# Scan stage of a four-layer image network: whole decays in PSUM, channel-group order, transposed attention

## The chip, the cores and the metric

The kernel runs on one core of one Trainium2 chip, in one launch. Its metric is the device time of that core in microseconds. Three executions of the kernel before took 13820.34 to 13844.27 us, median 13823.51; one further execution was profiled.

## The reference

64 images of 128 channels x 28 x 28 pixels (784 positions) in fp32 pass through four layers.

- Layer 0: two quantised 3x3 convolutions, each with a batch norm over all 64 images.
- Layer 1: attention inside each image. `scores = q^T k` (16 rows deep, 784 x 784), softmax along each row, values times weights, `gamma * out + x`.
- Layer 2: a Mamba block over the 784 positions of an image, in four reading directions: `h = exp(d*A)*h + d*u*B` for 160 inner channels x 24 states, `y = sum_n C*h`, plus `D*u`, times `silu(z)`, an output product, a mixing product, a residual.
- Layer 3: a small Mamba block over 8 tokens inside every pixel, group norm, silu, residual.

## The kernel before

`conv_block` runs first: batch norm needs all images before layer 1 may begin. `attention_and_mamba` (layers 1 and 2, here called the scan stage) follows, then `token_mamba` (layer 3). The change is in the scan stage alone.

**Units.** One image's scan has 160 x 24 = 3840 rows of 784 positions, 30 tiles of 128 partitions: a unit holds 32 channels (channel group q of NQ = 5) times 4 states (state group g of NG = 6). Units run in the order g outer, q inner (`at(n)`). For each unit:

- `inject` (GpSimd): `h = ur * Br`, the rows of d*u for group q, each on 4 x 32 partitions, times the rows of B for group g. It runs AHEAD = 5 units early; the h tiles number 10.
- `decay` (ScalarE): `a = exp(A * dr)`.
- `scan` (VectorE): one `tensor_tensor_scan` runs the recurrence along 784 positions. For q = 1 and 3 (`whole`) the decay lies in SBUF, up to three units ahead, and one instruction does 784; for q = 0, 2, 4 the decay is made in halves of 392 in PSUM (tile `ah`, 2 buffers) and two scans follow each other in `ah`.
- product with C: GpSimd for q = 1, 3 in g < 5 (10 of 30 units), VectorE for the others, in halves where the scan was.
- `sums` (TensorE): `fold` adds the 4 states of each channel into the PSUM tile `y`, which collects an image's 160 channels (channels 0 to 127 as 128 x 784, the last 32 as quarters over the partitions) over all six g. At the end VectorE multiplies `y` with the gate z in one instruction (`yo`, in `after`), and the output product follows.

**Rows.** `rows_bc` and `rows_d` fetch the rows of B, C, d and d*u from DRAM, spread over partitions in four transfers of 98 KB each, issued by SyncE. The B and C tiles have 2 buffers and are fetched one g ahead, the d and d*u tiles have 5.

**Side work.** While image b is scanned, three generators advance a few steps per unit (`side`): `attention` two to three images ahead, `inputs` (layer norm, input product, causal convolution as shifted products, softplus, silu) of image b+1, and `after` of image b−1. Attention takes 112 rows of scores at a time in a two-bank PSUM tile `wide`: row maximum (VectorE, `nmax`), exp with its row sum (ScalarE, `e`), seven transposes on TensorE copied out by ScalarE (`et`), the product with `vt` in seven pieces of 128 columns, a scaling copy (`avn`), a transpose back and the residual (`x`).

**Order.** Nothing is issued while this code runs. A `Plan` records each instruction with its reads, writes and pool buffers, `cost` gives each a length, and `Plan.order` lists them by a greedy simulation over five in-order queues (TensorE, VectorE, ScalarE, GpSimd, SyncE), for twelve settings of lead and patience, keeping the shortest; the scan chain has a lower rank (`plan.first()`) and so goes first among what is ready. All instructions are issued from one line, L493, so the profile is read by tile names.

**PSUM.** Eight banks: `bank` 2, `wide` 2, `ah` 2, `y` 2.

## Time and profile before

| | |
|---|---|
| median of 3 runs | 13823.51 us |
| profiled execution | 13818.13 us (span 13816.2) |
| granted TensorE clock, mean | 0.845 |
| VectorE busy | 12431.7 us (90%) |
| GpSimd busy | 11433.1 us (83%) |
| ScalarE busy | 10845.5 us (78%) |
| TensorE busy | 10467.5 us (76%) |
| DMA | 1297.64 MB, 94 GB/s |
| first nmax of the scan stage / last yo | about 683 us / 7738.4 us |

Engines are written PE (TensorE), PEld (its weight loads), DVE (VectorE), ACT (ScalarE), POOL (GpSimd) and SP (SyncE). A group's line names engine, operation, output tile `<-` input tiles, shapes and count, then busy time and mean length, then idle time of the engine just before such instructions and what ended it. A product of fp32 data stands as two matmul records. Lengths of neighbouring instructions of one engine overlap a little, since the next begins while the last one drains. Shares over the whole span mix three stages: the stretch from 3000 to 6000 us is the scan stage alone.

### The profile page before, as it was taken

Reading aid. Unit: us, or ns where it says so; the run is one execution under the profiler, and the core shown is the slowest. Engines: PE = TensorE matmul, PEld = TensorE weight load, DVE = VectorE, ACT = ScalarE, POOL = GpSimd, SP = SyncE. Lnnn points to the kernel's source line nnn. Section 1 sums busy time; section 2 is a strip of 40 time slices with the busy share of each in tenths; the row PEclk is TensorE's granted clock in tenths of the full one; section 3 lists DMA queues with packets and bytes.
Section 4 is the critical chain, followed back from the end, with each engine's and each line's share of the span. In section 5 each row is a group of like instructions: output and inputs, shape, how many; then the busy total and the mean of one; then the engine's idle time right before and its main releaser. Section 6 shows DMA issues by size and latency. Waiting matters only on the chain. (4 is left out here: it accounts for less than half of the span.)

```text
span 13816.2 us, 181376 instructions
## 1 busy us (share of the span) xinstructions
PE 10467.5 (76%) x58370; PEld 7153.8 (52%) x58370; DVE 12431.7 (90%) x12740; ACT 10845.5 (78%) x25904; POOL 11433.1 (83%) x5304
## 2 busy tenths in 40 slices
PE   9877777777777777777777577777767677777776
PEld 9644444444444444444443355656556565565564
DVE  3569999999999999999999799999999999999998
ACT  2367777777777777777777688888888888888887
POOL 0058999888988889898889788888888888888887
PEclk9988888888888888888888788888888888888887
DMA  3534444444444444444443211111111111121111
GB/s 129 186 93 128 124 125 125 133 126 126 123 125 130 129 125 122 126 126 132 129 122 120 74 49 54 51 52 60 44 54 49 56 56 46 51 63 46 52 51 46
DMA packets 711515, 1297.64 MB, mean 94 GB/s; under 512 B 206624, under 2 KB 357536, under 8 KB 710560
## 3 DMA queue, kind: packets, MB, share of 16 engines
q1 hardware_dynamic: 710560, 1286.05, 30.5%
q8 instruction: 460, 7.54, 0.2%
q14 instruction: 495, 4.06, 0.1%
HBM read 954.72 MB, written 330.76 MB: 93 GB/s over the span
## 5 line engine op out<-in xcount | busy, mean ns | idle before, releaser
L493 ACT ACTIVATE a<-delta,A 128x98 f32<-128x98 f32 x14336 | 3905.0, 366 | 764.7 <-PE y L493 545.2
L493 POOL TENSOR_TENSOR h<-ur,Br 128x784 f32<-128x784 f32 x1920 | 4196.7, 2211 | 138.9 <-PE y L493 122.0
L493 POOL TENSOR_TENSOR db<-u,BC 128x896 f32<-128x896 f32 x1568 | 3275.8, 2114 | 131.6 <-DVE h L493 125.5
L493 PE MATMUL y<-a,ident 128*128 128x280 f32 x7168 | 2059.4, 452 | 702.3 <-DVE a L493 701.2
L493 DVE TENSOR_TENSOR_SCAN ah<-ah,h 128x392 f32<-128x392 f32 x2304 | 2303.6, 1000 | 60.7 <-ACT ah L493 49.2
L493 PEld LDWEIGHTS y<-a,ident 128*128 128x128 f32 x7168 | 1554.0, 220 | 1223.4 <-issue 406.4
L493 DVE TENSOR_TENSOR_SCAN h<-a,h 128x784 f32<-128x784 f32 x768 | 1917.7, 2502 | 97.3 <-ACT a L493 54.2
L493 ACT ACTIVATE ah<-dr,A 128x392 f32<-128x392 f32 x2304 | 1322.7, 587 | 617.0 <-DVE ah L493 604.3
L493 POOL TENSOR_TENSOR h<-h,Cr 128x784 f32<-128x784 f32 x640 | 1362.0, 2132 | 354.2 <-DVE h L493 342.1
L493 DVE TENSOR_TENSOR h<-h,a 128x896 f32<-128x896 f32 x1344 | 1476.6, 1099 | 43.0
L493 DVE TENSOR_TENSOR h<-ah,Cr 128x392 f32<-128x392 f32 x2304 | 1302.6, 565 | 72.8
L493 PE MATMUL y<-h,fold 128*32 128x98 f32 (+1 forms) x12288 | 1023.3, 420 | 392.5 <-DVE h L493 366.7
L493 DVE TENSOR_TENSOR h<-h,db 128x896 f32<-128x896 f32 x1120 | 1230.3, 1098 | 94.1 <-POOL db L493 11.4
L493 PEld LDWEIGHTS bank<-vt,et 112*112 112x112 f32 x6272 | 892.1, 212 | 235.7 <-ACT et L493 88.7
L493 DVE TENSOR_TENSOR a<-h,BC 128x896 f32<-128x896 f32 x896 | 976.8, 1090 | 28.8
L493 PE MATMUL bank<-vt,et 112*112 112x128 f32 x6272 | 968.3, 317 | 6.6 <-ACT et L493 2.8
L493 POOL TENSOR_TENSOR xn<-s,sq 128x784 f32<-128x784 f32 x64 | 135.8, 2122 | 873.5 <-ACT sq L493 808.3
L493 PEld LDWEIGHTS y<-h,fold 128*32 128x32 f32 x12288 | 383.3, 121 | 910.4 <-DVE h L493 436.8
L493 PEld LDWEIGHTS y<-late,ident 128*128 128x128 f32 x7168 | 832.4, 192 | 23.2 <-issue 6.5
L493 ACT ACTIVATE a<-dr,A 128x784 f32<-128x784 f32 x768 | 716.9, 942 | 154.9 <-DVE h L493 147.9
L493 PE MATMUL y<-late,ident 128*128 128x112 f32 x7168 | 836.5, 274 | 0.0
L493 POOL TENSOR_TENSOR a<-a,db 128x896 f32<-128x896 f32 x224 | 530.0, 2366 | 309.6 <-issue 239.4
(212 smaller groups left out, 20910.5 us busy)
## 6 DMA issues: line engine op xcount, KB each, us to landing
Br<-bcd SPq DMA_DIRECT2D x1536, 98.0 KB, 2.4
Cr<-bcd SPq DMA_DIRECT2D x1536, 98.0 KB, 2.4
dr<-dud SPq DMA_DIRECT2D x1280, 98.0 KB, 2.3
ur<-dud SPq DMA_DIRECT2D x1280, 98.0 KB, 2.3
utd<-tok SPq DMA_DIRECT2D x128, 392.0 KB, 2.8
ztd<-tok SPq DMA_DIRECT2D x128, 392.0 KB, 3.7
rows<-utd SPq DMA_DIRECT2D x192, 256.0 KB, 2.9
xt<-in_x SPq DMA_DIRECT2D x32, 784.0 KB, 4.9
```

Of the source, the lines that this page charges most:

```text
L493: last = getattr(getattr(nc, engine), method)(*args, **kw)
```

## The change

- Units run q outer, g inner. The row tiles follow: all six B and all six C tiles stay for an image (6 buffers each), the d and d*u tiles have 2.
- Every decay is a whole one of 784 in a PSUM tile `a` of two banks, 2 buffers, made one unit ahead; every scan is one instruction. Where VectorE multiplies with C, the state stays in `a`; where GpSimd does, the scan writes `h` in SBUF. GpSimd takes g = 1, 3 and, for q = 1, 3, g = 5: 12 of 30 units. The h tiles number 9.
- `y` is one bank with the 32 channels of one q as four quarters; after the six g of a q, VectorE multiplies it with z (now laid out by q) into its piece of `yo`. The output product takes `yo` in 20 pieces, 64 rows deep, with the packed weight `Wout`.
- Attention: q and k get a 17th row, k's of ones. A first pass of scores gives row maxima in halves (`mx`), whose negatives (`nm`) go through a transpose, ScalarE and DRAM into q's 17th row. A second pass computes the scores transposed, already less the maxima, so that exp (`et`) yields the weights in the layout that the product with `vt` needs: seven products of 392 columns for each half. Row sums come from products with ones (`den`), reciprocals as exp(−ln) (`rq`), spread by products with `first_row` (`rd`). The bias of v is added at the end with the residual (`gbv`).
- PSUM: `bank` 3, `a` 4, `y` 1. The planner's costs for TensorE columns and GpSimd elements go from 0.0023 to 0.0021 us.

The diff, cut to its core; the removed lines of attention and sums are among the functions above.

```diff
         if engine == "tensor":
             if kw.get("is_transpose"):
                 return 0.18, False, 0.25
-            if outs[0].partition_size() == 32 or ins[0].partition_size() == 16:
+            if outs[0].partition_size() == 32:
+                return max(0.1, 0.03 + 0.0005 * n), False, 0.25
+            if ins[0].partition_size() in (16, 17):
                 return 0.03 + 0.0005 * n, False, 0.25
...
-        plan = Plan(tc, 0.0023, 0.0023, True)
+        plan = Plan(tc, 0.0021, 0.0021, True)
...
-        pss = plan.pool(ctx.enter_context(tc.tile_pool(name="pss3", bufs=1, space=PSUM)), 1)
-        psb = plan.pool(ctx.enter_context(tc.tile_pool(name="psb3", bufs=2, space=PSUM)), 2)
-        psh = plan.pool(ctx.enter_context(tc.tile_pool(name="psh3", bufs=1, space=PSUM)), 1)
+        psb = plan.pool(ctx.enter_context(tc.tile_pool(name="psb3", bufs=3, space=PSUM)), 3)
+        psa = plan.pool(ctx.enter_context(tc.tile_pool(name="psa3", bufs=2, space=PSUM)), 2)
         psy = plan.pool(ctx.enter_context(tc.tile_pool(name="psy3", bufs=1, space=PSUM)), 1)
-        def wide_psum():
-            return pss.tile([C, 2, 512], F32, name="wide")
...
+            x0 = p2.tile([C, T], F32, name="x0")
             plan.vector.tensor_scalar(x0, raw, MAGIC, 1.0 / 15.0, ALU.subtract, ALU.mult)
...
+            qt = p1.tile([49, T], F32, name="qt")
+            kt = p1.tile([49, T], F32, name="kt")
+            k0 = VEC_AT["bk"][0]
             for h in range(2):
...
+                acc = bank()[:113, :HT]
+                product(acc, [(w("WqkT"), x0[:, HALF[h]])])
+                act(qt[:, HALF[h]], acc[0:49], AF.Identity, bias=v("bq", p=49))
+                act(kt[:, HALF[h]], acc[64:113], AF.Identity, bias=vec[64:113, k0 : k0 + 1])
+            yield
...
+            rows16 = [slice(32 * h, 32 * h + 16) for h in range(2)]
+            rows17 = [slice(32 * h, 32 * h + 17) for h in range(2)]
+            mx = p1.tile([TP, NT, 2], F32, name="mx")
+            for i in range(NT):
+                sc = [bank()[:TP, :HT] for h in range(2)]
+                for h in range(2):
+                    plan.tensor.matmul(
+                        sc[h], lhsT=qt[rows16[h], i * TP : (i + 1) * TP], rhs=kt[rows16[h], HALF[h]],
+                        start=True, stop=True,
+                    )
+                for h in range(2):
+                    plan.vector.tensor_reduce(mx[:, i, h : h + 1], sc[h], AX.X, ALU.max)
+                yield
+            nm = p1.tile([TP, NT], F32, name="nm")
+            plan.vector.tensor_reduce(nm, mx, AX.X, ALU.max, negate=True)
+            tr = bank()[:NT, :TP]
+            plan.tensor.matmul(tr, lhsT=nm, rhs=ident[:TP, :TP], start=True, stop=True)
+            nmt = p1.tile([NT, TP], F32, name="nmt")
+            act(nmt, tr, AF.Copy)
+            nmd = rows_dram.tile([NT, TP], F32, name="nmd")
+            plan.sync.dma_start(nmd, nmt)
+            for h in range(2):
+                plan.sync.dma_start(qt[32 * h + 16 : 32 * h + 17, :], nmd.rearrange("(o a) c -> o (a c)", o=1))
+            yield
+            x1 = p2.tile([C, T], F32, name="x1")
+            for h in range(2):
+                et = []
+                for j0 in range(0, NT, 2):
+                    js = range(j0, min(j0 + 2, NT))
+                    sc = [bank()[:TP, :HT] for _ in js]
+                    for j in js:
+                        rows = rows17[j % 2]
+                        plan.tensor.matmul(
+                            sc[j - j0], lhsT=kt[rows, j * TP : (j + 1) * TP], rhs=qt[rows, HALF[h]],
+                            start=True, stop=True,
+                        )
+                    for j in js:
+                        e = p1.tile([TP, HT], F32, name="et", bufs=8)
+                        act(e, sc[j - j0], AF.Exp)
+                        et.append(e)
+                    yield
+                den = bank()[:, :ET]
+                for j in range(NT):
                     with plan.together():
...
+                        for k in range(4):
                             plan.tensor.matmul(
...
+                                den[32 * k : 32 * k + 32], lhsT=ones, rhs=et[j][:, k * ET : (k + 1) * ET],
+                                start=(j == 0), stop=(j == NT - 1), skip_group_check=True,
                             )
...
+                rq = p2.tile([C, ET], F32, name="rq")
+                act(rq, den, AF.Ln)
+                act(rq, rq, AF.Exp, scale=-1.0)
                 yield
...
+                acc = bank()[:, :HT]
+                with plan.together():
+                    for k in range(4):
+                        plan.tensor.matmul(
+                            acc[:, k * ET : (k + 1) * ET], lhsT=first_row[:, k : k + 1].broadcast_to([C, C]), rhs=rq,
+                            start=(k == 0), stop=True, skip_group_check=True,
+                        )
+                rd = p2.tile([C, HT], F32, name="rd")
+                act(rd, acc, AF.Copy)
+                av = bank()[:, :HT]
+                for j in range(NT):
+                    plan.tensor.matmul(av, lhsT=vt[:, j, :], rhs=et[j], start=(j == 0), stop=(j == NT - 1))
+                plan.vector.scalar_tensor_tensor(x1[:, HALF[h]], av, v("att_gamma"), rd, ALU.mult, ALU.mult)
                 yield
...
+            plan.vector.scalar_tensor_tensor(x1, x1, gbv, x0, ALU.add, ALU.add)
             plan.sync.dma_start(x1d[b % 4], x1)
...
-            z = p2.tile([C, 2, HW2], F32, name="z", bufs=3)
+            z = p2.tile([C, NQ, QT], F32, name="z", bufs=3)
...
-            for h in range(2):
-                acc = bank()[:, :HT]
-                product(acc, [(winz[:, :C], shifted[3][:, HALF[h]])])
-                act(z[:, h, :HT], acc, AF.Identity, bias=bias[:, 0, 1:2])
+            for q0 in (0, 2):
+                acc = bank()
+                for k in range(2):
+                    q = q0 + k
+                    quarters(
+                        acc[:, k * QT : (k + 1) * QT], [(winz[:, 32 * q : 32 * q + 32], shifted[3])], first=(k == 0)
+                    )
+                    act(z[:, q, :], acc[:, k * QT : (k + 1) * QT], AF.Identity, bias=biasz[:, q : q + 1])
...
-        def rows_bc(b, g):
+        def rows_bc(b, g, k):
             bcd = given[b][2]
-            for k, name in enumerate("BC"):
-                t = p2.tile([C, T], F32, name=f"{name}r", bufs=2)
-                n = 24 * k + 4 * g
-                spread(t, lambda r: bcd[n + r : n + r + 1, :].broadcast_to([32, T]))
-                rows_of[name, b, g] = t
+            name = "BC"[k]
+            t = p2.tile([C, T], F32, name=f"{name}r", bufs=NG)
+            n = 24 * k + 4 * g
+            spread(t, lambda r: bcd[n + r : n + r + 1, :].broadcast_to([32, T]))
+            rows_of[name, b, g] = t
         def rows_d(b, q, k):
             name = ("dr", "ur")[k]
-            t = p2.tile([C, T], F32, name=name, bufs=NQ)
+            t = p2.tile([C, T], F32, name=name, bufs=2)
             spread(t, lambda r: given[b][3][k, 32 * q : 32 * q + 32, :])
             rows_of[name, b, q] = t
-        def after(b, ys):
-            z = given.pop(b)[1]
+        def after(b, yo):
+            given.pop(b)
...
             for h in range(2):
                 acc = bank()[:, :HT]
-                product_q(acc, h, w("WoutA"), lambda j: w("WoutB", j * C, (j + 1) * C), yo)
+                rows = slice(64 * h, 64 * h + 64)
+                for q in range(NQ):
+                    with plan.together():
+                        for k in range(2):
+                            at = (2 * q + k) * C
+                            plan.tensor.matmul(
+                                acc[:, k * QT : (k + 1) * QT], lhsT=w("Wout", at, at + C)[rows], rhs=yo[rows, q, :],
+                                start=(k == 0 and q == 0), stop=(q == NQ - 1), skip_group_check=True,
+                            )
...
-        def whole(g, q):
-            return q in (1, 3)
+            q, g = divmod(n, NG)
+            return b, g, q
         def on_gpsimd(g, q):
-            return q in (1, 3) and g < 5
+            return g in (1, 3) or (g == 5 and q in (1, 3))
         def inject(n):
             b, g, q = at(n)
             if n == 0:
-                rows_bc(0, 0)
-                for i in range(NQ):
+                for i in range(2):
                     for k in range(2):
                         rows_d(0, i, k)
-            h = hs[n] = st.tile([C, T], F32, name="h", bufs=10)
+                for i in range(NG):
+                    for k in range(2):
+                        rows_bc(0, i, k)
+            h = hs[n] = st.tile([C, T], F32, name="h", bufs=9)
             plan.gpsimd.tensor_tensor(h, rows_of["ur", b, q], rows_of["B", b, g], ALU.mult)
-            if q == 0:
-                nxt = (b, g + 1) if g + 1 < NG else (b + 1, 0)
+            if g == NG - 1:
+                nxt = divmod(b * NQ + q + 2, NQ)
                 if nxt[0] < NB:
-                    rows_bc(*nxt)
-            if g == NG - 1 and b + 1 < NB:
-                rows_d(b + 1, q, 1)
-        def decay(n, hf=None):
+                    rows_d(*nxt, 1)
+            if q == NQ - 1 and b + 1 < NB:
+                rows_bc(b + 1, g, 0)
+        def decay(n):
             b, g, q = at(n)
-            k, dr = g * NQ + q, rows_of["dr", b, q]
-            if hf is None:
-                a = st.tile([C, T], F32, name="a", bufs=4)
-            else:
-                a, dr = psh.tile([C, 512], F32, name="ah", bufs=2)[:, :HT], dr[:, HALF[hf]]
-            decays[n, hf] = a
-            act(a, dr, AF.Exp, scale=A[:, k : k + 1])
-            if hf != 0 and g == NG - 1 and b + 1 < NB:
-                rows_d(b + 1, q, 0)
-        def scan(n, hf=None):
+            k = g * NQ + q
+            a = decays[n] = psa.tile([C, 1024], F32, name="a")[:, :T]
+            act(a, rows_of["dr", b, q], AF.Exp, scale=A[:, k : k + 1])
+            if g == NG - 1:
+                nxt = divmod(b * NQ + q + 2, NQ)
+                if nxt[0] < NB:
+                    rows_d(*nxt, 0)
+        def scan(n):
             b, g, q = at(n)
-            a, h, Cr = decays.pop((n, hf)), hs[n], rows_of["C", b, g]
-            since = 0.0
-            if hf is not None:
-                h, Cr = h[:, HALF[hf]], Cr[:, HALF[hf]]
-            state = h if hf is None or on_gpsimd(g, q) else a
-            if hf == 1:
-                since = states.pop(n)
-            elif hf == 0:
-                states[n] = state[:, HT - 1 : HT]
-            plan.vector.tensor_tensor_scan(state, a, h, since, ALU.mult, ALU.add)
-            if not on_gpsimd(g, q):
-                plan.vector.tensor_tensor(h, state, Cr, ALU.mult)
-            elif hf != 0:
-                h = hs[n]
-                plan.gpsimd.tensor_tensor(h, h, rows_of["C", b, g], ALU.mult)
+            a, h, Cr = decays.pop(n), hs[n], rows_of["C", b, g]
+            state = h if on_gpsimd(g, q) else a
+            plan.vector.tensor_tensor_scan(state, a, h, 0.0, ALU.mult, ALU.add)
+            engine = plan.gpsimd if on_gpsimd(g, q) else plan.vector
+            engine.tensor_tensor(h, state, Cr, ALU.mult)
+            if q == NQ - 1 and b + 1 < NB:
+                rows_bc(b + 1, g, 1)
         def sums(n):
             b, g, q = at(n)
...
+            u, z = given[b][:2]
+            if g == 0:
+                y = yps[b] = psy.tile([C, 512], F32, name="y")[:, :QT]
                 with plan.together():
...
+                    if q < NQ - 1:
+                        for j in range(4):
+                            lo = (j % 2) * QT
                             plan.tensor.matmul(
...
+                                y[32 * j : 32 * j + 32], lhsT=DA[:, 32 * q : 32 * q + 32],
+                                rhs=u[:, j // 2, lo : lo + QT], start=True, stop=False, skip_group_check=True,
                             )
...
+                    else:
+                        plan.tensor.matmul(
+                            eighths(y), lhsT=DB, rhs=u[:, :, HT:], start=True, stop=False, skip_group_check=True
+                        )
+            y, h = yps[b], hs.pop(n)
+            with plan.together():
+                for j in range(4):
+                    plan.tensor.matmul(
+                        y[32 * j : 32 * j + 32], lhsT=fold, rhs=h[:, j * QT : (j + 1) * QT],
+                        start=False, stop=(g == NG - 1), skip_group_check=True,
+                    )
+            if g == NG - 1:
+                if q == 0:
+                    yos[b] = p2.tile([C, NQ, QT], F32, name="yo", bufs=1)
+                plan.vector.tensor_tensor(yos[b][:, q, :], y, z[:, q, :], ALU.mult)
...
-                if 0 <= n + 3 < total and whole(*at(n + 3)[1:]):
-                    decay(n + 3)
-                if n >= 0 and whole(*at(n)[1:]):
+                if 0 <= n + 1 < total:
+                    decay(n + 1)
+                if n >= 0:
                     scan(n)
-                for hf in range(2):
-                    if n >= 0 and not whole(*at(n)[1:]):
-                        scan(n, hf)
-                    if 0 <= n + 1 < total and not whole(*at(n + 1)[1:]):
-                        decay(n + 1, hf)
                 if n >= 0:
                     sums(n)
```

## The prediction

> **What bounds the kernel now.** I read the page's busy shares, then the busy time by stretches, then the groups of instructions in the stretch from 3000 to 6000 us, then the timeline of single engines. The scan stage lies between about 690 and 7770 us: VectorE's tile yo, written once an image, first appears at 937.72 and last at 7738.36, so an image takes (7738.36 − 937.72) / 63 = 107.9 us. The columns below are the stretch, then busy us (instructions) of TensorE, its weight loads, VectorE, ScalarE, GpSimd, then granted clock, DMA share, GB/s.
>
> ```profile
> 0.00:1200.00 1200.00, 1039.15 (x5969) 788.16 (x5969) 665.58 (x907) 584.39 (x824) 350.45 (x169) 0.92 0.40 134
> 3000.00:6000.00 3000.00, 2356.70 (x14629) 1340.73 (x14623) 2892.06 (x3214) 2358.28 (x3855) 2687.15 (x1219) 0.85 0.41 126
> ```
>
> The second row holds 832 injections (next fence), 30 an image: 27.7 images. VectorE is busy 2892.06 / 27.7 = 104.3 of 108.2 us an image and bounds; GpSimd 96.9, ScalarE and TensorE 85.0 each. In the groups (count | busy us, mean ns | idle before) the reader is to see which shapes VectorE pays for:
>
> ```profile
> L493 POOL TENSOR_TENSOR h<-ur,Br 128x784 f32<-128x784 f32 x832 | 1813.6, 2205 | 44.5 <-PE y L493 44.5
> L493 DVE TENSOR_TENSOR_SCAN ah<-ah,h 128x392 f32<-128x392 f32 x996 | 995.8, 1000 | 14.6 <-ACT ah L493 11.0
> L493 DVE TENSOR_TENSOR_SCAN h<-a,h 128x784 f32<-128x784 f32 x332 | 819.1, 2473 | 37.3 <-ACT a L493 26.9 <-POOL h L493 6.6
> L493 DVE TENSOR_TENSOR h<-ah,Cr 128x392 f32<-128x392 f32 x997 | 563.6, 565 | 31.5
> L493 ACT ACTIVATE a<-dr,A 128x784 f32<-128x784 f32 x332 | 310.2, 942 | 58.7 <-DVE h L493 58.0
> L493 DVE TENSOR_REDUCE nmax<-wide 112x1 f32<-112x784 f32 x196 | 187.6, 957 | 1.7 <-PE wide L493 0.6
> L493 DVE TENSOR_TENSOR yo<-y,z 128x980 f32<-128x980 f32 x28 | 32.7, 1168 | 0.0
> ```
>
> A whole scan with both inputs in SBUF averages 2.473 us, yet two half scans with the decay in PSUM take 2.000. The timelines say why: the same SBUF scan takes 1.78 us while GpSimd stands still and 3.17 at worst here, and GpSimd's product takes 1.84 or 3.32.
>
> ```profile
> 4001.06 1.78 DVE L493 TENSOR_TENSOR_SCAN h<-a,h 128x784 f32<-128x784 f32 x1
> 934.62 3.17 DVE L493 TENSOR_TENSOR_SCAN h<-a,h 128x784 f32<-128x784 f32 x1
> 4016.03 1.84 POOL L493 TENSOR_TENSOR h<-h,Cr 128x784 f32<-128x784 f32 x1
> 4046.07 3.32 POOL L493 TENSOR_TENSOR h<-h,Cr 128x784 f32<-128x784 f32 x1
> ```
>
> VectorE and GpSimd hold each other up where VectorE reads two SBUF tensors; half scans (0.96 to 1.04) do not show it. The products of C say the same by their tiles' view (least, median and most ns): flat with the state in PSUM, up to 2642 with both in SBUF.
>
> ```profile
> L493 DVE TENSOR_TENSOR h<-ah,Cr x997: 547/566/569, 2999.8 to 5996.3; 128x392 f32<-128x392 f32 x200
> L493 DVE TENSOR_TENSOR h<-h,Cr x54: 962/967/2642, 3086.3 to 5905.7; 128x784 f32<-128x784 f32 x54
> ```
>
> **The change, part by part, per image.**
>
> VectorE removed, from those rows and their neighbours: 36 half scans x 1.000, 12 whole scans x 2.473, 36 half products x 0.565, 2 whole products x 1.457, 7 nmax x 0.957, 7 rden x 0.148, 7 x1 pieces x 0.316, two vt (0.667, 0.538), yo 1.168: 101.2 us, 110 instructions.
>
> Added: 30 whole scans from PSUM. The trace has none; the ends are 1.78 (quiet SBUF scan) and 2.00 (two halves). The fixed part of an instruction, from products of 392 (0.565) and of 896 elements (token stage, 1.099), is 0.15, so 2.000 − 0.15 = 1.85; I take it, 55.5 us. 18 products x 0.98 (0.565 plus 392 elements at 1.06 ns) 17.6; 14 reductions of 392 x 0.54, 7.6; nm 0.15; two x1 halves at 0.62; one whole x1 from two SBUF tiles, between 0.97 quiet and 2.73 (raw), taken as 2.0; five yo pieces of 196 at 0.34, 1.7: 85.8 us, 71 instructions.
>
> The rows' means overlap: together they exceed the busy time by 0.05 us an instruction, so 39 fewer give back 2.0. Net −13.4: VectorE goes from 104.3 to 90.9 us.
>
> GpSimd keeps 30 injections and has 12 products for 10. With only five VectorE instructions an image left that read two SBUF tensors or hold it up, its price is the quiet 1.84: 42 x 1.84 + xn 1.85 + pos, pos, ab 8.8 = 88.0, less 0.04 overlap each, plus up to 4 for those five: 88 to 91, from 96.9. It runs level with VectorE.
>
> ScalarE loses 36 x 0.587 and 12 x 0.942 for decays, 7 x 2.45 for exp, read-out and copies of the old attention, and gains 30 decays (0.95), 14 exps of 392 (0.49), copies and logarithms (about 8): net −8, to 77. Eight more table loads (1.28 us) stand in the two attentions ahead of the first scan, where nothing covers them: +10, with the transposed pass in series +15 in all.
>
> A decay is now one unit ahead instead of three for the whole ones. ScalarE works in order: in the changed order up to 8 us of other activations lie between two decays (abs, relu and r copies; sums of 0.42 to 1.03), and 5 to 6 us for a silu with its two table loads. Two PSUM tiles cover two units, 2 x 2.8; the rest is VectorE's side work, which stands in the same places (raw, eight reductions, ab: 9.8 us in a row). I leave 1.5 us an image.
>
> TensorE, from bursts in its timeline:
>
> ```profile
> 4021.38 1.77 PE L493 MATMUL bank<-vt,et 112*112 112x128 f32 x14
> 4025.16 1.52 PE L493 MATMUL y<-h,fold 128*32 128x392 f32 x16
> 4027.03 1.58 PE L493 MATMUL bank<-x,wxc 128*128 128x392 f32 x4 [0.35 <-DVE x L493]
> 4029.16 0.92 PE L493 MATMUL wide<-kt,qt 16*112 16x392 f32 x4
> 4030.44 0.55 PE L493 MATMUL y<-h,fold 128*32 128x98 f32 x16
> ```
>
> A product shows as two matmul records. Removed: 7 x 1.77 (values), 7 x 1.05 (transposes) and 7 x 0.31, 6 x 1.52 and 6 x 0.55 (y). Added: 14 x 0.79 (values), 8 more score pairs x 0.92, 14 denominators x 0.28, 30 y sums of 196 columns between 0.28 and 0.76, taken as 0.5, small row spreads 1.6, and the output product in 20 pieces of 0.40 (before 5.4 in all). Removed 39.8, added 47: net +7, between 0 and +15 with the ends of the y price. TensorE comes to 92 of 96.5 us, nearly full. VectorE now waits for it at 5 yo pieces, 14 reductions and 2 x1 halves instead of 1, 7 and 7; behind each stand the next scan, its product and GpSimd's product. VectorE idles 3.9 us an image now; I take 5.6.
>
> SyncE: the same 88 row transfers of 98 KB an image, plus three small ones. B and C rows of the next image now go out in the last channel group, 8 a unit: 784 KB in 3.2 us is 245 GB/s against 126 at a 41% share, an estimated 80%. Each is wanted six units (19 us) later and lands in 2.4, so I cost it at nothing; without that slack 5 us an image. The round trip of the maxima through DRAM lies in attention, which ends some 29 units before it is used.
>
> The sum: 90.9 + 5.6 = 96.5 us an image, 107.9 − 96.5 = 11.4, times 63 = −718, +15 ahead of the scans, against the profiled execution's 13818.1: 13115; the median of the runs lies 5 above it, so 13120.
>
> [...] The rows: 0.92 granted where TensorE is 87% busy, 0.85 where 79%. [...]
>
> **The rivals.** (1) Everything hides: idle stays 3.9 or less, period 90 to 93.5, 12740 to 12930. For it: fewer instructions, no lock. Against: two other engines near full.
> (2) TensorE or ScalarE sets the pace, period 99.5 to 104.5: 13310 to 13620. For it: TensorE at 92 us. Against: busy there includes modelled ends and slow-clock stretches.
> (3) The lock stays, because scans that GpSimd multiplies still write SBUF: 12 x 0.6 on VectorE and GpSimd's products nearer 2.2 (42 x 0.36 = 15): period 102 to 106, 13440 to 13720. Against: half products with one SBUF input and an SBUF output stay at 0.565.
> (4) Slower: decays no longer run ahead. If ScalarE's 0.94 stood before every scan, 30 x 0.94 on 90.9 gives 119 us, 14530. It decides from (107.9 − 90.9) / 30 = 0.57 us exposed per unit. Against: VectorE waited for ScalarE 38 us of 3000 now.
>
> **How the numbers follow.** Forecast (93.5 to 99.5 us an image, 12930 to 13310) 0.55; (1) 0.12; (2) 0.17; (3) 0.08; (4) 0.07, and 0.01 for no change, which is within 0.2%, what this measurement can tell. Faster 0.92, same 0.01, slower 0.07. The range 12860 to 13540 holds the forecast, a third of (1), three quarters of (2) and a part of (3): 0.8.
>
> **What would show it.** Right: whole scans a<-a,h and h<-a,h near 1.85 us alike, GpSimd's h near 1.84 with few at 3.3, VectorE over 92% busy, yo of channel group 4 some 96 us apart. Wrong: VectorE's waits for PE (yo, mx) or for ACT a above 10 us an image; scans writing h near 2.4; GpSimd busy above VectorE.

## The result, and the profile after

The changed kernel takes 13900.22 us (median of four runs, 13892.22 to 13908.83) against 13826.35 beside it: a ratio of 1.0051, 95% interval 1.0034 to 1.0069. It is 0.5% slower; the forecast was 5% faster. The profiled execution took 13908.83 us (span 13907.0).

Where the time went is read from VectorE's tile yo, whose fifth piece ends an image: the first image is done at 1001.55 us (937.72 before), the last at 7833.35 (7738.36), and what follows takes 6074 us (6078). So 64 us are lost ahead of the first image and (6831.8 − 6800.6) = 31 in the 63 that follow: the period is 108.4 us an image, as good as unchanged, where 96.5 was forecast.

Busy time by stretches, of the kernel after (columns as in the prediction):

```profile
3000.00:6000.00 3000.00, 2715.84 (x18829) 1466.96 (x18828) 2471.29 (x2118) 2104.59 (x3098) 2348.38 (x1260) 0.81 0.42 125
```

With 820 injections this row holds 27.33 images, 109.8 us each. VectorE is busy 90.4 us an image (104.3 before; 90.9 forecast) and idle 19.3 (3.9 before; 5.6 forecast). GpSimd has 85.9, ScalarE 77.0, TensorE 99.4 (85.0 before; 92 forecast), and the granted clock fell from 0.85 to 0.81 while TensorE works more. Groups of the same stretch, after:

```profile
L495 POOL TENSOR_TENSOR h<-ur,Br 128x784 f32<-128x784 f32 x820 | 1506.6, 1863 | 126.7 <-issue 63.8 <-PE y L495 62.9
L495 DVE TENSOR_TENSOR_SCAN a<-a,h 128x784 f32<-128x784 f32 x492 | 877.2, 1783 | 3.9 <-ACT a L495 0.9 <-POOL h L495 0.5
L495 DVE TENSOR_TENSOR_SCAN h<-a,h 128x784 f32<-128x784 f32 x329 | 586.2, 1782 | 199.6 <-ACT a L495 196.6 <-POOL h L495 3.0
L495 DVE TENSOR_TENSOR h<-a,Cr 128x784 f32<-128x784 f32 x491 | 477.1, 972 | 13.2
L495 DVE TENSOR_REDUCE mx<-bank 112x1 f32<-112x392 f32 x392 | 206.3, 559 | 231.4 <-PE bank L495 229.8
L495 DVE SCALAR_TENSOR_TENSOR x<-x,gbv,x 128x784 f32<-128x784 f32 x28 | 193.3, 6903 | 0.0
L495 PE MATMUL bank<-kt,qt 16*112 16x392 f32 x784 | 325.7, 843 | 31.3 <-ACT r L495 27.3 <-DVE mx L495 3.9
L495 PE MATMUL bank<-qt,kt 17*112 17x392 f32 x756 | 272.8, 626 | 8.6 <-DVE x L495 7.3
L495 PE MATMUL bank<-yo,pk 64*128 64x196 f32 x1115 | 356.4, 487 | 0.0
```

All scans take 1.78 us, whether they write PSUM or SBUF: what the change was to do to VectorE's instructions, it does. What stands against it is in the last two columns. VectorE's waits, after (us of 3000, times, longest):

```profile
DVE mx L495 <- PE bank L495: 229.8, 159, 3.4
DVE h L495 <- ACT a L495: 196.6, 80, 3.9
DVE yo L495 <- PE bank L495: 68.9, 28, 2.5
DVE yo L495 <- PE y L495: 10.4, 27, 1.0
```

That is 8.4 us an image at the reductions of the first pass of scores, 7.2 at decays and 2.9 at the yo pieces. (yo has one buffer, so its first piece waits for the output product of the image before.) The timelines show both kinds. TensorE, after, from 3998 us:

```profile
3998.82 1.65 PE L495 MATMUL bank<-kt,qt 16*112 16x392 f32 x4
4001.72 5.26 PE L495 MATMUL bank<-kt,qt 16*112 16x392 f32 x12 [1.24 <-ACT r L495]
4006.90 6.90 PE L495 MATMUL bank<-yo,pk 64*128 64x196 f32 x20
4013.73 1.65 PE L495 MATMUL bank<-kt,qt 16*112 16x392 f32 x4
```

VectorE, after, over the same time:

```profile
4000.50 1.04 DVE L495 TENSOR_REDUCE mx<-bank 112x1 f32<-112x392 f32 x2 [3.38 <-PE bank L495]
4003.40 1.04 DVE L495 TENSOR_REDUCE mx<-bank 112x1 f32<-112x392 f32 x2 [1.85 <-PE bank L495]
...
4013.84 0.36 DVE L495 TENSOR_TENSOR yo<-y,z 128x196 f32<-128x196 f32 x1 [2.46 <-PE bank L495]
...
4020.55 0.57 DVE L495 TENSOR_REDUCE mx<-bank 112x1 f32<-112x392 f32 x1 [2.02 <-PE bank L495]
```

A pair of score halves arrives every 1.65 us (0.92 in the burst of before that the prediction took its price from), the output product's second half takes 6.9 us in one piece, and VectorE stands 1.85 to 3.38 us ahead of these rows, with the next scan behind each. And ScalarE, after, ahead of two late decays (VectorE waited 3.45 us at 4049.38 and 3.03 at 4057.28):

```profile
4042.20 1.28 ACT L495 ACT_TABLE_LOAD   x1
4043.49 3.10 ACT L495 ACTIVATE tok<-tok 128x784 f32<-128x784 f32 x4
4046.61 1.28 ACT L495 ACT_TABLE_LOAD   x1
...
4052.84 0.88 ACT L495 ACTIVATE et<-bank 112x392 f32<-112x392 f32 x2 [1.14 <-PE bank L495]
4054.56 0.88 ACT L495 ACTIVATE et<-bank 112x392 f32<-112x392 f32 x2 [0.83 <-PE bank L495]
4055.87 0.50 ACT L495 ACTIVATE et<-bank 112x392 f32<-112x392 f32 x1 [0.42 <-PE bank L495]
4056.26 1.75 ACT L495 ACTIVATE a<-dr,A 128x784 f32<-128x784 f32 x2
```

Of VectorE's idle time ahead of the scans that write `h` in this stretch (200 us), ScalarE spends 71 on the decay itself, 49 on exp for attention, 35 on table loads and 17 on the silu of `tok`: for half of it, it is working on other things. VectorE stood idle from 4045.93 for the first of the two, and that decay started at 4048.38, behind the rest of the silu, a table load and two `rq`.

### The profile page after: what moved, and what is told of

Its sections match the earlier page's. It is cut to its first block, busy times and chain, and to the rows that moved or that the text cites. A ratio compares the mean times of both kernels' runs of the same rounds, so it can differ in the third digit from the quotient of the medians.

```text
span 13907.0 us, 199754 instructions
## 1 busy us (share of the span) xinstructions
PE 11389.6 (82%) x68768; PEld 7485.9 (54%) x68768; DVE 11502.3 (83%) x10248; ACT 10318.4 (74%) x24248; POOL 10715.8 (77%) x5432
## 5 line engine op out<-in xcount | busy, mean ns | idle before, releaser
L495 POOL TENSOR_TENSOR h<-ur,Br 128x784 f32<-128x784 f32 x1920 | 3529.9, 1866 | 335.8 <-PE y L495 159.3
L495 ACT ACTIVATE a<-dr,A 128x784 f32<-128x784 f32 x1920 | 1737.5, 915 | 702.0 <-DVE h L495 635.8
L495 DVE TENSOR_TENSOR_SCAN a<-a,h 128x784 f32<-128x784 f32 x1152 | 2053.9, 1783 | 72.6 <-ACT a L495 45.5
L495 DVE TENSOR_TENSOR_SCAN h<-a,h 128x784 f32<-128x784 f32 x768 | 1368.3, 1782 | 444.6 <-ACT a L495 427.5
L495 PE MATMUL y<-h,fold 128*32 128x196 f32 x15360 | 1085.4, 394 | 195.9 <-DVE h L495 140.1
L495 DVE TENSOR_TENSOR h<-a,Cr 128x784 f32<-128x784 f32 x1152 | 1119.3, 972 | 31.5 <-DMA Cr<-bcd 0.3
L495 DVE TENSOR_REDUCE mx<-bank 112x1 f32<-112x392 f32 x896 | 472.0, 559 | 511.0 <-PE bank L495 506.7
L495 PE MATMUL bank<-yo,pk 64*128 64x196 f32 x2560 | 805.7, 486 | 0.6 <-DVE yo L495 0.5
L495 PE MATMUL bank<-kt,qt 16*112 16x392 f32 x1792 | 741.5, 840 | 68.6 <-ACT r L495 59.6
L495 PEld LDWEIGHTS bank<-yo,pk 64*128 64x128 f32 x2560 | 667.2, 284 | 221.2 <-issue 141.3
```

The lines of the kernel that those rows point to most:

```text
L495: last = getattr(getattr(nc, engine), method)(*args, **kw)
```

## The experiments

Four suspects: the one whole residual x1, 6.9 us an image instead of 2.0 (A); TensorE's busy time as such (B); the half clock in attention's thin products (C); three work banks (D). Later came the decays: a cause of their own, or a consequence? Every ratio is to the kernel before on the same chip; runs on different chips are compared by their ratios, a hundredth being 138 us. The period is from yo; idle is VectorE's, in us an image, from the stretch 3000 to 6000 us (3000 less its busy time, by the images of that stretch).

| run | median us | ratio (95%) | period | idle |
|---|---|---|---|---|
| the change | 13900.22 | 1.0051 (1.0034 to 1.0069) | 108.4 | 19.3 |
| e1_x1_psum | 13722.24 | 0.9926 (0.9911 to 0.9941) | 105.4 | 19.0 |
| e2_wout_pairs | 14076.96 | 1.0187 (1.0170 to 1.0204) | 111.2 | 20.1 |
| e3_no_max | 13104.96 | 0.9477 (0.9460 to 0.9495) | 97.1 | 14.6 |
| e4_attention_only | 14468.68 | 1.0472 (1.0452 to 1.0492) | 117.8 | 13.6 |
| e5_pairs1 | 14055.26 | 1.0161 (1.0146 to 1.0176) | 110.7 | 19.6 |
| e6_costs | 13878.61 | 1.0033 (1.0021 to 1.0045) | 108.3 | 19.5 |
| e7_thick_max | 14090.29 | 1.0183 (1.0168 to 1.0198) | 111.3 | 22.7 |
| e8_best1 | 13169.19 | 0.9517 (0.9501 to 0.9533) | 98.1 | 20.3 |
| e9_max128 | 13726.62 | 0.9926 (0.9911 to 0.9940) | 105.7 | 18.9 |
| e10_bank2 | 14489.13 | 1.0476 (1.0461 to 1.0492) | 117.4 | 31.8 |
| e11_no_toksilu | 13071.42 | 0.9454 (0.9440 to 0.9468) | 96.6 | 13.7 |
| e12_split_silu | 13052.71 | 0.9438 (0.9423 to 0.9454) | 96.0 | 17.5 |
| e13_h7 | 14083.58 | 1.0182 (1.0166 to 1.0198) | 112.1 | 25.4 |
| e14_sbuf_decays3 | 16535.98 | 1.1949 (1.1929 to 1.1969) | 149.4 | 13.5 |
| e15_sbuf_decays7 | 16470.97 | 1.1904 (1.1886 to 1.1922) | 149.3 | 9.1 |
| e16_const3 | 13709.97 | 0.9910 (0.9894 to 0.9927) | 105.7 | 16.7 |
| e17_const5 | 13403.44 | 0.9693 (0.9674 to 0.9711) | 100.5 | 11.4 |
| e18_const5_no_max | 13151.41 | 0.9506 (0.9492 to 0.9520) | 98.2 | 16.7 |

### Which half of the change is which

**e4: the new attention in the old scan.** Units in the old order with half scans, h with nine tiles, four work banks.

> The scan of the kernel before (h 9 instead of 10 buffers) with the new attention alone. If the new attention carries the loss: TensorE up by some 12 us an image, the same long slow stretch of the clock, x1 long: 14000 to 14400. If the new scan does (whole decays one unit ahead, y by channel group): within 50 of the kernel before, 13770 to 13880.

It is 646 us slower than before, above its band. With the new scan on top it is 74: under the new attention the new scan is worth 0.0421 (1.0472 − 1.0051), 582 us, although e4 has four work banks and the change three. The change is a gain and a loss of about one size; the new scan under the old attention was not run.

**e3: no first pass.** The score products for the maxima, the reductions, the transpose and its trip through DRAM go; the softmax is unshifted.

```diff
-            for i in range(NT):
-                sc = [bank()[:TP, :HT] for h in range(2)]
...
-                    plan.vector.tensor_reduce(mx[:, i, h : h + 1], sc[h], AX.X, ALU.max)
```

> Leaves out the row maxima of attention: no first pass of scores, no reductions, no round trip through DRAM; the softmax is unshifted. Theory A: VectorE loses 8.4 us of waits and 6.8 of reductions an image: about 12950, granted clock unchanged at 0.81 to 0.82. Theory B: TensorE loses 11.9 us an image: about 13150, clock unchanged. Theory C, the 16-row matmuls of the first pass bring the half clock that lasts 27 us once an image: the long slow stretches vanish, the clock is at least 0.85 in the scan stage, and the time is at 12900 or below.

13104.96, 0.0574 under the change: 793 us, 11.3 us of period. VectorE's own work there (14 reductions and nm) is 7.7 us an image; the waits went as well, yet 14.6 us of idle time stay, now 8.6 of them at decays. Theory B's time is nearest: the clock stays at 0.82, although the longest stretch at half clock falls from 34 to 20 us. Stretch of e3:

```profile
3000.00:6000.00 3000.00, 2751.79 (x20267) 1550.20 (x20266) 2553.21 (x1906) 2309.03 (x3423) 2655.86 (x1412) 0.82 0.46 140
```

### A: the lock at x1

**e1.** The scaling by the row sums stays in PSUM, and the residual is added from there in halves.

```diff
-                plan.vector.scalar_tensor_tensor(x1[:, HALF[h]], av, v("att_gamma"), rd, ALU.mult, ALU.mult)
+                plan.vector.scalar_tensor_tensor(av, av, v("att_gamma"), rd, ALU.mult, ALU.mult)
+                plan.vector.scalar_tensor_tensor(x1[:, HALF[h]], av, gbv, x0[:, HALF[h]], ALU.add, ALU.add)
...
-            plan.vector.scalar_tensor_tensor(x1, x1, gbv, x0, ALU.add, ALU.add)
```

> The whole x1 instruction (6.9 us, two SBUF inputs) is replaced by two halves that read the attention product from PSUM (0.6 us each). Theory A, VectorE's stalls once an image (x1 5.9, mx 8.4, yo 2.5, decays 7.0 us) add up one by one: 5.7 us an image less, 63 images, about 13540. Theory B, TensorE (99 of 109.8 us busy) sets the period whatever VectorE does: 13840 to 13900, with longer VectorE waits elsewhere.

173 us under the change, half of what A expected. The reason is in e1's groups: the wait moved to the next SBUF instruction, x0's multiply, 0.57 us in the changed kernel:

```profile
L495 DVE TENSOR_SCALAR x<-raw 128x784 f32<-128x784 f32 x28 | 106.1, 3790 | 0.0
```

**e8: e3 and e1 together.**

> Without the row maxima and with the x1 halves read from PSUM. If the two gains add (795 and 178): 12930. [...]

55 us slower than e3 alone, and above the expected 12930: the gains don't add. Nor did the wait move to x0's multiply, which takes 0.57 us in e8. VectorE's work fell, from 83.3 to 79.0 us an image, and its idle time rose, from 14.6 to 20.3. In e2 below, too, x1 is only 1.24 us, and the kernel is slower.

### B: TensorE's busy time

**e2.** The output product's two 64-row halves alternate in two banks instead of following each other in one.

```diff
-            for h in range(2):
-                acc = bank()[:, :HT]
+            accs = [bank()[:, :HT] for h in range(2)]
```

> The output product's pieces for the upper and the lower 64 rows alternate, so that two row groups can run at once; 13.0 us of TensorE time an image. Theory A: only the yo wait (2.5 us an image) goes, about 13740. Theory B: TensorE's busy time falls by some 6 us an image and the period with it, about 13520. If the pieces do not run together: 13900, and the matmul records stay one behind the other.

In e2's groups the product shrinks from 13.0 us of TensorE an image to 5.5 (147.0 / 26.9):

```profile
L495 PE MATMUL bank<-yo,pk 64*128 64x196 f32 x1080 | 147.0, 397 | 0.0
```

The kernel is 188 us slower, and e2's first wait on VectorE grew by a third:

```profile
DVE mx L495 <- PE bank L495: 299.4, 265, 3.4
```

That does not acquit TensorE's busy time, since TensorE as a whole hardly got lighter, 98.2 us an image (2641.63 / 26.9) for 99.4: other products grew, the first pass from 11.9 to 13.7. Stretch of e2:

```profile
3000.00:6000.00 3000.00, 2641.63 (x18472) 1266.66 (x18471) 2458.10 (x2054) 2057.02 (x3024) 2309.96 (x1233) 0.81 0.41 123
```

What speaks against busy time as such are later runs: from e3 to e11 TensorE loses 6.0 us an image (89.7 to 83.7) and the period 0.5, from e17 to e18 9.6 (91.7 to 82.1) and 2.3. That e2 is slower because two of three banks are held at once fits e10 below, but was not isolated.

**e5: score halves in pairs** (both products of a pair issued together) and **e6: the planner's cost of the scores doubled** (`0.03 + 0.0005 * n` to `0.06 + 0.0011 * n`).

> The two score products of a row block in the first pass are planned as one step, so that they start together on two groups of rows, and wait until two banks are free. If the first pass costs because its products run one by one (11.9 us of TensorE an image instead of the 6.4 of my sum): mx waits fall from 8.4 to about 3 us an image, 13550 to 13650. If three banks are the limit, as the slower run with two banks held by the output product suggests: 13850 or above.

> Only the planner's length for a 16- or 17-row product goes from 0.23 to 0.49 us; the work is the same, the order differs. If the written order is too hopeful about the scores and VectorE therefore stands before reductions: mx waits halve, 13600 to 13750. If not: 13850 to 13950.

e5 is 152 us slower than the change, with 3.97 us of VectorE's wait an image at scores instead of 8.4 and more at decays, yo and x; e6 is 25 us faster, and the intervals overlap. Waits change places in both, and neither brings the period down: neither is the cause.

### C: the clock

In the changed kernel the clock stands at half in 1161 of 3000 us (872 before), with a run of 27 to 34 us once an image in which TensorE hardly pauses (95% busy). 85% of the first pass's products were issued at half clock, 70% of the output product's, 3% of the values' (112 rows deep). Depth alone does not sort them: it is 25% for the second pass (17 rows) and 95% for the product with `centre_w` (128 rows).

**e7: 48 rows** instead of 16 in the first pass (scores doubled, undone in `nmt`), and **e9: 128 rows** (x0 times x0 in place of q times k, so the softmax is shifted by other numbers).

```diff
-                        sc[h], lhsT=qt[rows16[h], i * TP : (i + 1) * TP], rhs=kt[rows16[h], HALF[h]],
+                        sc[h], lhsT=qt[0:48, i * TP : (i + 1) * TP], rhs=kt[0:48, HALF[h]],
```

> The first pass contracts over 48 rows instead of 16 (both copies of q and k, so twice the score; the maxima are halved). Same instructions, columns and waits. Theory C, products of few rows bring the long half-clock stretch: first-pass products fall from 0.65 towards 0.33 us a record, granted clock up by 0.02 or more, 13550 to 13750. If the rows do not matter: 13850 to 13950.

> The first pass multiplies x0 with itself over 128 rows instead of q with k over 16; columns, instructions, banks and reductions stay. (Each row is then shifted by another number, which the softmax does not see.) Theory C, refined: a busy TensorE whose products fill few rows or columns runs at half clock; full ones bring the full clock back. Against the 48-row kernel (14090, slow stretches of 34 to 37 us): first-pass records at 0.33 instead of 0.65 us, slow stretches below 15 us, granted clock in the scan stage 0.84 or more, time 13600 to 13800. If the rows do not matter: 14050 to 14130 and the same long stretches.

Stretch of e7, then of e9:

```profile
3000.00:6000.00 3000.00, 2756.40 (x18512) 1442.94 (x18510) 2392.30 (x2053) 2042.14 (x3035) 2317.14 (x1231) 0.80 0.40 123
DVE mx L495 <- PE bank L495: 278.4, 234, 3.6
```

```profile
3000.00:6000.00 3000.00, 2663.60 (x19476) 1386.07 (x19477) 2465.55 (x2166) 2150.95 (x3188) 2438.10 (x1298) 0.89 0.43 130
DVE mx L495 <- PE bank L495: 108.5, 78, 3.6
```

The same instructions and the same columns, 128 rows against 48: 355 us faster (1.0183 − 0.9926), half clock in 635 us of 3000 instead of 1186, VectorE's wait for scores 108.5 instead of 278.4, though its wait for y rose from 91.0 to 209.6. The clock is very likely a cause; what was not separated is that e9's first pass, made from x0, no longer waits for q and k. That 48 rows were worse than 16 (182 us) has not been explained; one rival is the order, since the planner's `cost` knows only 16 and 17 rows and takes a first-pass product as 0.88 us in e7 and e9 alike, 0.23 in the change.

### D: the banks

**e10: two work banks** (`psb`, `bufs=3` to `bufs=2`).

> Two banks instead of three for everything TensorE hands to the side work; the third stays empty. Theory D, banks limit the scan stage (65 tiles an image pass through three): 14400 or above. If they do not: 13850 to 14000, and the two slower runs that held two banks at once were slower for another reason.

588 us slower than the change; VectorE idles 31.8 us an image. Fewer banks cost much. Whether more would help needs room, and decays in SBUF give four banks.

**e13: seven state tiles** for nine, four units ahead, which frees the SBUF; **e14: e13 with the decays in SBUF**; **e15: e14 with seven work banks.**

```diff
-            a = decays[n] = psa.tile([C, 1024], F32, name="a")[:, :T]
+            a = decays[n] = st.tile([C, T], F32, name="a", bufs=2)
```

> The control for the next two runs: the changed kernel with 7 state tiles instead of 9, and injections four units ahead instead of five, which frees the SBUF that decays need there. If the states run far enough ahead (VectorE waited for an injection 3.5 us of 3000 in the changed kernel), it keeps its time within 1%: 13830 to 14040 us. If the fifth unit was the cover of GpSimd's runs of injections, VectorE's waits for GpSimd's h rise above 60 us of 3000 and the time above 14040.

> The control, with the decays written to SBUF (two tiles, one unit ahead as before), and the three work banks of PSUM kept. Theory that the decay in PSUM is what took the lock away: the scans rise from 1.78 to 2.3 to 2.5 us, 30 an image, 15 to 21 us more on VectorE, and GpSimd's injections from 1.86 to 2.1 or more; the waits for the first pass of scores hide a part: 14300 to 15100 us. Rival, that the scans were quick because few products with two SBUF inputs stand beside them, whatever the decay's place: scans stay under 1.9 and the time within 1% of the control.

> The same with decays in SBUF, and the four banks that they leave given to the work banks: seven instead of three. Theory that the banks limit attention (two instead of three cost 589 us): VectorE's wait for the first pass of scores falls from 230 us of 3000 to under 80, ScalarE's waits for banks fall too, and the run is 300 us or more below the one with three banks. Theory that the half clock of the thin products alone makes the pass late: the products still come one by one at about 0.84 and 0.62 us a record, the waits for scores stay above 150 us of 3000, and the two runs agree within 100 us. If the first holds, the change paid for its decays in PSUM with the banks that its attention needed.

e13 missed its band: two state tiles and the fifth unit ahead are worth 181 us, seen as VectorE's waits for y (8.9 us an image). e14 missed on the far side: the period rises by 37 us. Its groups show what had been left out of the expectation, that the states move to SBUF too, and with them VectorE's products:

```profile
L495 POOL TENSOR_TENSOR h<-ur,Br 128x784 f32<-128x784 f32 x600 | 1642.3, 2757 | 133.4 <-PE y L495 92.6 <-DVE h L495 40.8
L495 DVE TENSOR_TENSOR_SCAN a<-a,h 128x784 f32<-128x784 f32 x360 | 1051.8, 2934 | 137.0 <-ACT a L495 137.0
L495 DVE TENSOR_TENSOR h<-a,Cr 128x784 f32<-128x784 f32 x359 | 723.3, 2040 | 2.1
L495 DVE TENSOR_TENSOR_SCAN h<-a,h 128x784 f32<-128x784 f32 x240 | 642.4, 2677 | 70.8 <-POOL h L495 49.5 <-ACT a L495 21.3
```

Scans go from 1.78 us to 2.68 and 2.93, products from 0.97 to 2.04, GpSimd's from 1.88 to 2.76. The decays (and with them the states) in PSUM are what takes the lock away. VectorE is the bound again (94% busy in e15), so the 62 us between e15 and e14 say nothing on banks.

### Decays and banks once more

**e16: no decays.** ScalarE makes none, every scan reads one constant column in PSUM, the states share one tile. **e17: the two banks this frees go to the work banks**, five for three. **e18: e17 without the first pass.**

```diff
-            act(a, rows_of["dr", b, q], AF.Exp, scale=A[:, k : k + 1])
...
+        half = only[:, 1023:1024].broadcast_to([C, T])
```

> The changed kernel without its decays: ScalarE computes none, every scan reads one constant column held in PSUM (so the outputs are another recurrence's), and the states of VectorE's units share one PSUM tile; three work banks as before. It takes 30 activations of 0.95 us an image from ScalarE and VectorE's wait for decays (7.2 us an image). Theory that late decays are a cause of their own: the 7.2 us go, 63 images x 7.2 = 450 us, to about 13450 us. Theory that they are a consequence of ScalarE standing before attention's banks: the waits move to mx and yo, which rise above 330 us of 3000 together, and the time stays above 13700 us.

> The same, with the two PSUM banks that are now free given to the work banks: five instead of three. Theory that the work banks limit attention: the waits for the first pass of scores fall below half of those with three banks, and the run is 300 us or more below it. Theory that the half clock and the serial thin products make the pass late, however many banks: the two agree within 100 us.

> The same with five banks, and without the first pass of scores and the maxima (softmax unshifted). All three suspected causes are gone: VectorE's busy time is about 83 us an image, and if nothing else delays it, it idles as the prediction said, 6 us an image or less: period 83 to 89, 12250 to 12640 us. If it idles above 10 us an image, a fourth cause is left, and the time is above 12900.

e16 gains 195 us on the change where 450 would say that late decays are a cause of their own. ScalarE has 26 us less to do an image, and VectorE's waits turn up elsewhere, as the theory of a consequence had it, if less at mx and yo (312 us where it said above 330). In e16:

```profile
DVE mx L495 <- PE bank L495: 212.5, 196, 1.8
DVE yo L495 <- PE bank L495: 99.4, 28, 3.6
DVE x L495 <- PE bank L495: 46.2, 28, 1.7
DVE h L495 <- POOL h L495: 45.7, 57, 1.1
```

e17 gains another 300 by banks alone, as the theory of banks said, but not where it said. In e17 the wait for the first pass is 7.4 us an image as against 7.5; it is the wait of yo that went:

```profile
DVE mx L495 <- PE bank L495: 221.0, 179, 3.0
DVE x L495 <- PE bank L495: 58.4, 66, 1.5
DVE a L495 <- POOL h L495: 19.4, 11, 1.8
```

e18 then should have left 6 us of idle time. It has 16.7, and is no faster than e3, which has its decays and three banks. No wait leads in e18:

```profile
DVE x L495 <- PE bank L495: 80.8, 30, 6.2
DVE h L495 <- DMA Cr<-bcd: 76.3, 60, 3.2
DVE a L495 <- POOL h L495: 68.6, 30, 5.8
DVE h L495 <- POOL h L495: 64.2, 40, 3.6
DVE raw L495 <- DMA raw<-c2d: 51.4, 7, 9.1
```

So there is a further loss of about 11 us an image that none of the suspects makes. Its cause was not isolated. GpSimd waits for the sums into y (148 us of 3000) and TensorE for yo (288), so the one buffer of y, which VectorE has to empty five times an image, is a candidate; it was not tried.

### Versions

**e11: e3 without the token branch's silu**, and **e12: e3 with that silu in two steps.**

```diff
-            silus(*(tok for tok, _ in toks))
+            silus(*(tok for tok, _ in toks[:2]))
+            yield
+            silus(*(tok for tok, _ in toks[2:]))
```

> On the kernel without row maxima (13105): the silu of the token tiles and its two table loads are left out, 5.9 us an image in which ScalarE makes no decay. If such blocks are what makes decays late (8.6 us of VectorE waits an image there): half of the waits go, 12830 to 12930. If decays are late because ScalarE waits for TensorE's banks ahead of them: 13050 to 13130.

> On the kernel without row maxima: the silu of the token tiles in two blocks of two tiles with two table loads each, 4.2 us instead of one of 5.9, for 2.6 us more ScalarE work an image. If the length of one block against the two units of decays made ahead (5.4 us) decides: 12950 to 13050. If ScalarE's total does: 13150 to 13250.

Leaving it out gains 32 us against e3, splitting it 54 (the intervals of the two overlap). e11 lies in the band of the theory that decays are late because ScalarE stands before TensorE's banks; the block of table loads and silus is a small part of the late decays, which cost 13.7 us an image in e12. e12 is the fastest run, 5.6% under before, with an unshifted softmax that rests on scores of a size that exp can take. Of those that keep both the maxima and the decays e1 is fastest, 0.7% under before.

## Why the prediction was wrong

**VectorE's work: right.** Scan 1.78 (1.85 taken, ends 1.78 and 2.00), products 0.972 (0.98), reductions 0.559 (0.54), sum 90.4 us an image (90.9). The whole x1 was mis-sized, 6.9 for 2.0 and outside its ends (0.97 to 2.73); two neighbours (raw 2.73 before and 1.01 after, ab 2.75 and 1.17) made up for most of it.

**GpSimd: right by the instruction**, 1.863 for 1.84, and 85.9 us for 88 to 91; pos, pos and ab took 6.8 us for 8.8, and the printed terms add up to 86 to 90. **ScalarE: 77.0 for 77**, with luck: the printed terms add up to −6, so 79.

**The step that failed: "VectorE idles 3.9 us an image now; I take 5.6."** It measured 19.3, and those 13.7 us are the whole miss of the period (109.8 − 96.5 = 13.3 in this stretch). The value was scaled from a kernel in which VectorE was busy 104 of 108 us and everything else ran ahead of it. With VectorE at 90 and three engines at 77 to 99, no variant idled under 9, and the two lowest (9.1, 11.4) were one with VectorE slowed again by the lock and one with the decays left out. The prediction had counted the places ("5 yo pieces, 14 reductions") and then raised the idle time by 1.7 us in all; with 1.5 of them for late decays, 0.2 were left for waits on TensorE that measured 11.3 (8.4 at the reductions, 2.9 at yo). So what failed is not the size of VectorE's work but the assumption that VectorE still bounds. Followed back from instruction to releaser through the stretch (releasers as the profile infers them), the chain of work spent 55% of its time in VectorE and 11% in TensorE before; after, it spends 45% in TensorE, 24% in VectorE and 14% in ScalarE. In e3 TensorE's share is 27%.

**TensorE: 99.4 for 92, inside its bounds (85 to 100) but badly split.** First and second pass 21.9 us for 13.8, output product 13.0 for 8.0: the prices came from bursts at full clock, 0.92 a pair (granted 1.0 at 4029.16 in before), and most of the first pass and of the output product ran at half. e9 against e7 shows the clock at work.

**Banks: no step at all.** Four of eight banks went to decays and three stayed for all side work. e10 puts 588 us on one bank less, e17 (without decays) 300 us on two more.

**Late decays: 1.5 taken, 7.2 measured.** e16 shows that they, and ScalarE's 26 us of work on them, count for 195 us; the rest is replaced by other waits when they go.

**The lead: 15 taken, 64 measured.** The two uncovered attentions lie there; e3 has its first image done at 913.87, 88 us earlier than the change, so it is the first pass again. **DMA rows at nothing: right** here for VectorE (Cr 0.3 us over the span), though e18 shows the slack used up once the period shortens.

**The rivals.** (1) fell. (2) foresaw a pace of 99.5 to 104.5 by TensorE: its 99.4 busy us and its share of the chain fit, the period of 108.4 does not, and e11 and e18 (under B) show that the period hardly follows TensorE's busy time alone; e2 does not decide it. (3) fell: scans that write h take 1.782 us, as the others. (4) had the sign, and even its price: it decides at 17 us of idle time an image beyond 90.9, and 19.3 came. But decays are only 7.2 of it. The low ends of (1) and (3) are slips of the sum: a period of 90 gives 12710 and not 12740, 102 gives 13466 and not 13440. And the whole scan's "3.17 at worst" is too low: the trace of before has 3.48 in the stretch.

**PSUM or SBUF, and the lock.** The rows show no price for a source in PSUM: 1.783 us for a scan with its decay there, 1.79 in before for the 24 whole scans, both inputs in SBUF, that no instruction of GpSimd overlaps. The lock is in the trace of before: in 294 of the stretch's 332 whole scans an instruction of GpSimd ends; these take 2.38 us and end 1.65 us after it (medians). The prediction's quiet row at 4001.06 is not one without GpSimd: `pos` runs beside it from 4001.21.

**Clock and load.** TensorE went from 79% to 91% busy and the granted clock from 0.85 to 0.81. The prediction had named the row at 0.85 and still priced TensorE by bursts at full clock.

## What to carry to other kernels

When an edit makes the bounding engine lighter, its idle time is not carried over from a profile in which it bounded: count each new place where it waits for another engine, price it at the mean or the slow end of that engine's rows of that shape and not at its best burst, and ask what stands behind. Price a stage's PSUM banks like an engine: who holds each for how long, and what is left for the rest. A large change is often a gain and a loss in one; here the scan was worth 582 us and the attention cost 646, which one run of a half alone shows.

## What the runs showed of the hardware that had not been expected

**One instruction can wait for a row of GpSimd's.** x1 reads two SBUF tiles. By its tile's view, after (least, median, most ns), it took 1.04 to 7.08 us:

```profile
L495 DVE SCALAR_TENSOR_TENSOR x<-x,gbv,x x64: 1035/6878/7081, 750.1 to 7580.2; 128x784 f32<-128x784 f32 x64
```

GpSimd's timeline, after, at the time when one of them ran from 3982.49 to 3989.50:

```profile
3979.53 9.13 POOL L495 TENSOR_TENSOR h<-ur,Br 128x784 f32<-128x784 f32 x5
```

VectorE got in only when the run of five injections had ended, not after the first of them. In the stretch this holds for all 27: four injections end inside x1, which takes 6.81 to 7.08 us and ends 0.83 us after the last of them. In e2, x1 takes 2.13 to 2.17 us where one injection ends inside it (5 times) and 1.03 to 1.04 where none does (22 times). The prediction's upper end, 2.73, fits the wait for a single one.

**TensorE at half clock while busy.** 27 to 44 us at a stretch (the changed kernel, e7, e10 and e16; 86 to 97% busy), mostly with thin products (of 16 and 64 rows in 72% of that time in the changed kernel), and 635 us of half clock in 3000 when the first pass used all 128 rows (e9) instead of 1186 with 48 (e7).

**Products in two row groups overlapped.** The 64-row output product took 5.5 us an image instead of 13.0 when its halves alternated in two banks (e2). A part of that is clock: 22% of its records were issued at half clock there, 70% in the changed kernel.
